# A joint tile of small slot groups in four column groups, and its stream rows gathered first into buffers of their own

## The chip, the cores and the metric

The kernel runs on one core of a Trainium2 chip. A core has TensorE (PE, the matrix unit; its weight loads are listed as PEld), VectorE (DVE), ScalarE (ACT), GpSimd (POOL) and SyncE (SP, which here only issues transfers), and 16 DMA engines that all queues share. Each engine works through its own instructions in order and waits for others by semaphores. The metric is the device time of one execution in microseconds. Before the change the median of three runs is 751.44 us (750.15 to 752.66).

## The reference

The input x holds 16 sequences of 128 tokens of width 256. Two blocks are added to it in turn: a cross-attention, and a feed-forward layer in which each token goes to one of eight experts and to a shared expert. The change touches the second block only. Cut to what matters:

```python
x = x + xcond(ctx_1024, layernorm(x), cond, cond, ...)    # attention, 16 heads of 64
h = layernorm(x)                                           # 2048 tokens of 256
scores = h @ router                                        # one of E = 8 experts, K = 1
vals, idx = top_k(scores, 1)
gates = sigmoid(vals at idx, -inf elsewhere)
routed_in = gates * h                                      # per expert
mid = silu(routed_in @ w1[e]) * (routed_in @ w3[e])        # F = 704
routed_out = mid @ w2[e]
shared = silu(h @ ws1) * (h @ ws3) @ ws2
x = x + shared + routed_out.sum over experts
```

All of it is in f32.

## The kernel before

The program is written with a manual schedule: on every engine, instructions run in the order in which the Python code issues them. Waits between engines, and waits for a buffer's earlier user, are put in by the framework.

The first some 510 us are the attention, with the first units of the shared expert mixed in. Then come the routing and the rest of the shared expert, and from about 585 us the eight expert windows, which the change is about.

**Slots and windows.** The routing (`route`, from L989) counts the tokens of each expert and sorts the experts by load. Window w is the w-th most loaded expert. The program has fixed room for each, in `WINDOWS` (L24): 320, 288, 288, 288, 256, 256, 256, 256 slots. The first 256 slots of a window are two tiles of 128 rows, tiles 2w and 2w + 1. What is over, `REST` = 64, 32, 32, 32 slots for windows 0 to 3, is put together in two joint tiles: tile 16 has window 0's 64 rows (rows 0 to 63), window 1's 32 (64 to 95) and window 2's 32 (96 to 127); tile 17 has window 3's 32 rows alone. The list `rests` (L1194 to L1198) holds for each joint tile the entries (window, first row, number of rows). `table` holds for each tile and row the token in it.

**Inputs.** `gather` (L1200) fetches a tile's rows of h from memory by an indirect DMA that GpSimd issues (tile `xg`, three buffers in the pool `rwork`). `gate` scales them on VectorE. For windows 1 to 7, `turn_inputs` turns them on VectorE in blocks of 32, writes them to memory through SP, and `fetch_inputs` reads them back as columns `xT`. The tiles of window 0 and the two joint tiles are transposed on TensorE instead (`transpose_inputs`, L1215), and VectorE copies the columns to the windows' inputs: one copy for an entry of `rests` (L1225).

**Up.** For each of six chunks f of the hidden width, `up` (L1268) computes the two products `u_w` on TensorE (eight matmul records; the last chunk, `ur_w`, has four), silu on ScalarE, and the product with the other half on VectorE (`mid_w`, L1286). `u_w` has two PSUM buffers, so a chunk can start on TensorE once VectorE's product (L1286) of the chunk two before it is done.

**Down.** `stream_rows` (L1292) gathers, with an indirect DMA of GpSimd, the rows of `s_rows` (x plus the shared expert's part) for a tile's tokens, into the tile `sg`. `out_rows` (L1304) multiplies the hidden tiles by w2 on TensorE (`yr`), six chunks of one matmul for an ordinary tile; for a joint tile each chunk has one matmul for each entry of `rests`, which writes that entry's rows of the output and so uses as many columns of the array (L1310). VectorE adds `sg` (L1313), and GpSimd scatters the rows to the output by an indirect DMA (L1315). Two scatters in a row are ordered: the later one waits for the earlier one to land.

The tile `sg` has the tag `xr` in the pool `mwork`, with three buffers, which the shared expert's tiles `xr` and later the last rows of the output (`held`) use too.

**The order in window w** (L1357 to L1378), all issued behind chunk f = 0 of its up products: the gathers of the stream rows of tiles 2w - 2 and 2w - 1; turning of the next window's inputs; the gathers of h for window w + 2; `down_window(w - 1)`, with its two adds and two scatters; in window 4 (w = `NREST`) `down_rests` for tiles 16 and 17, which issues for each the stream gather, the matmuls, the add and the scatter; then SP's transfers of inputs and weights. Chunks 1 to 5 follow. So GpSimd's queue in window 4 is: stream gathers of tiles 6 and 7, gathers of h for tiles 12 and 13, scatters 6 and 7, stream gather 16, scatter 16, stream gather 17, scatter 17. On VectorE the four adds stand ahead of the product of chunk f = 1.

At the end, `ending` (L1380) does the last eighth of the shared expert and window 7's down products. A second branch, for loads that don't fit the windows, is compiled and is not entered with these inputs.

Of the kernel before, what the change touches and what calls it, by code (L numbers as in the profile page):

```python
# [9 lines left out]
F32 = mybir.dt.float32  # L10
# [7 lines left out]
P = 128  # L18
# [9 lines left out]
def resampler_attn__then__top1_moe_kernel(  # L28
# [17 lines left out]
    nc = tc.nc  # L46
    B, S, D = x.shape
    INNER = wq_t.shape[1]
    E, F = w1.shape[0], w1.shape[2]
# [12 lines left out]
    BL = 32  # L62
# [4 lines left out]
    REST = [n - 2 * P for n in WINDOWS]  # L67
    NREST = sum(r > 0 for r in REST)
    NTILE = 2 * E - (-sum(REST) // P)
# [8 lines left out]
    mwork = ctx.enter_context(tc.tile_pool(name="mwork", bufs=2, side="right"))  # L78
# [176 lines left out]
    def shared_unit():  # L255
        return next(stream, None)
# [653 lines left out]
    rwork = ctx.enter_context(tc.tile_pool(name="rwork", bufs=3))  # L910
# [7 lines left out]
    w2s = [wexp.tile([P, NF, D], F32, name=f"w2_{k}") for k in range(5)]  # L918
# [70 lines left out]
    def route():  # L989
# [191 lines left out]
        for t in first[:3]:  # L1181
            transpose_inputs(t)
# [3 lines left out]
        for t in first[3:]:  # L1186
            transpose_inputs(t)
# [3 lines left out]
    inputs_t = [rwork.tile([P, DC, WMAX], F32, name=f"xT_{k}", bufs=1) for k in range(NREST)]  # L1191
    x_blocks = tc.dram_tile([DC, 2 * NB, BL, NB, BL], F32, name="x_blocks")

    rests = [[] for _ in range(NTILE - 2 * E)]  # L1194
    for w in range(NREST):
        at = sum(REST[:w])
        assert at // P == (at + REST[w] - 1) // P
        rests[at // P].append((w, at % P, REST[w]))  # L1198

    def gather(t, tag="xg"):  # L1200
        xg = rwork.tile([P, D], F32, tag=tag, name=f"xg_{t}")
        nc.gpsimd.indirect_dma_start(
            out=xg,
            out_offset=None,
            in_=h_rows,
            in_offset=Offset(ap=routing["table"][:, t : t + 1], axis=0),
            bounds_check=NT,
            oob_is_err=False,
        )
        xgs[t] = xg  # L1210
# [4 lines left out]
    def transpose_inputs(t, to=None):  # L1215
        xg = xgs.pop(t)
        px = ps_m.tile([P, DC, P], F32, tag="mm", name=f"px_{t}")
        for c in range(DC):
            nc.tensor.transpose(px[:, c, :], xg[:, ts(c, P)], ident)
        if to is None and t < 2 * E:  # L1220
            to = inputs_t[t // 2][:, :, ts(t % 2, P)]
        if to is not None:
            nc.vector.tensor_copy(to, px)
            return
        for w, at, n in rests[t - 2 * E]:  # L1225
            nc.vector.tensor_copy(inputs_t[w][:, :, ds(2 * P, n)], px[:, :, ds(at, n)])

    def turn_inputs(w):

        for i in range(2):  # L1230
            t = 2 * w + i
            gate(t)
            px = rwork.tile([P, DC, NB, BL], F32, tag="xp", name=f"xp_{t}")
            nc.vector.transpose(px, xgs.pop(t).rearrange("p (c k j) -> p c j k", c=DC, k=BL))
            nc.sync.dma_start(
                out=x_blocks[:, ts(i, NB)].rearrange("c i k j q -> (i k) c (j q)"),
                in_=px.rearrange("p c j q -> p c (j q)"),
            )

    def fetch_inputs(w):  # L1240
        for c in range(DC):
            nc.sync.dma_start(
                out=inputs_t[w % NREST][:, c, 0 : 2 * P].rearrange("p (i q) -> p i q", q=BL),
                in_=x_blocks[c].rearrange("i k j q -> (k j) i q"),
            )
# [4 lines left out]
    def load_up(k, w):  # L1250
        e = expert_of(w)
        a1, a3 = (a[ds(e, 1)].rearrange("e (c p) f -> p (e c) f", p=P) for a in (w1, w3))
        nc.sync.dma_start(out=w13s[k][:, :, 0:F], in_=a1)
        nc.sync.dma_start(out=w13s[k][:, :, F : F + FR], in_=a3[:, :, FC * P : F])
        nc.sync.dma_start(out=w13s[k][:, :, F + FR : 2 * F], in_=a3[:, :, 0 : FC * P])

    def load_down(k, w):
        e = expert_of(w)
        a2 = w2[ds(e, 1)]
        nc.sync.dma_start(  # L1260
            out=w2s[k][:, 0:FC, :],
            in_=a2[:, 0 : FC * P, :].rearrange("e (c p) d -> p (e c) d", p=P),
        )
        nc.sync.dma_start(
            out=w2s[k][:, FC, :], in_=a2[:, F - P : F, :].rearrange("e p d -> p (e d)")
        )

    def up(w13, xT, n, mid, f, name):  # L1268

        if f < FC:  # L1270
            ps = ps_s.tile([P, 2, 512], F32, tag="S", name=f"u_{name}_{f}")
        else:
            ps = ps_m.tile([P, 1, 512], F32, tag="mm", name=f"ur_{name}")
        sl = mwork.tile([P, WMAX], F32, tag="sl", name=f"rsl_{name}_{f}")[:, 0:n]
        for k, col in enumerate((f * P, F + FR + f * P) if f < FC else (FC * P,)):
            for c in range(DC):
                nc.tensor.matmul(  # L1277
                    ps[:, k, 0:n],
                    lhsT=w13[:, c, ds(col, P)],
                    rhs=xT[:, c, 0:n],  # L1280
                    start=(c == 0),
                    stop=(c == DC - 1),
                )
        if f < FC:
            nc.scalar.activation(sl, ps[:, 0, 0:n], AF.Silu)  # L1285
            nc.vector.tensor_tensor(mid[:, f, 0:n], ps[:, 1, 0:n], sl, ALU.mult)  # L1286
        else:
            hi = slice(P - FR, P)
            nc.scalar.activation(sl[hi, :], ps[0:FR, 0, 0:n], AF.Silu)
            nc.vector.tensor_tensor(mid[hi, FC, 0:n], ps[hi, 0, 0:n], sl[hi, :], ALU.mult)  # L1290

    def stream_rows(t):  # L1292
        sg = mwork.tile([P, D], F32, tag="xr", name=f"sg_{t}", bufs=3)
        nc.gpsimd.indirect_dma_start(  # L1294
            out=sg,
            out_offset=None,
            in_=s_rows,
            in_offset=Offset(ap=routing["table"][:, t : t + 1], axis=0),
            bounds_check=NT,
            oob_is_err=False,  # L1300
        )
        return sg

    def out_rows(t, parts, sg):  # L1304

        py = ps_m.tile([P, D], F32, tag="mm", name=f"yr_{t}")
        n = max(r.stop for r, _, _ in parts)
        for f in range(NF):
            for rows, mid, wd in parts:
                nc.tensor.matmul(  # L1310
                    py[rows, :], lhsT=mid[:, f, :], rhs=wd[:, f, :], start=(f == 0), stop=(f == NF - 1)
                )
        nc.vector.tensor_tensor(sg[0:n, :], py[0:n, :], sg[0:n, :], ALU.add)  # L1313
        scattered.append(
            nc.gpsimd.indirect_dma_start(  # L1315
                out=out.rearrange("b s d -> (b s) d"),
                out_offset=Offset(ap=routing["table"][0:n, t : t + 1], axis=0),
                in_=sg[0:n, :],
                in_offset=None,
                bounds_check=NT - 1,  # L1320
                oob_is_err=False,
            )
        )
# [13 lines left out]
    mids = [hidden_t.tile([P, NF, WMAX], F32, name=f"mid_w{k}") for k in range(5)]  # L1337
# [3 lines left out]
    def down_window(w, sgs):  # L1341
        for i in range(2):
            out_rows(2 * w + i, [(slice(0, P), mids[w % 5][:, :, ts(i, P)], w2s[w % 5])], sgs[i])

    def down_rests():
        for k, parts in enumerate(rests):
            t = 2 * E + k
            out_rows(
                t,
                [  # L1350
                    (slice(at, at + n), mids[w][:, :, ds(2 * P, n)], w2s[w])
                    for w, at, n in parts
                ],
                stream_rows(t),
            )

    for w in range(E):  # L1357
        for f in range(NF):
            up(w13s[w % 3], inputs_t[w % NREST], WINDOWS[w], mids[w % 5], f, f"w{w}")
            if f == 0:  # L1360
                sgs = [stream_rows(2 * w - 2 + i) for i in range(2)] if w else []
                if w + 1 < E:
                    turn_inputs(w + 1)
                if w + 2 < E:
                    gather(2 * w + 4)
                    gather(2 * w + 5)
                if w:
                    down_window(w - 1, sgs)
                else:
                    shared_unit()  # L1370
                if w == NREST:
                    down_rests()
                if w + 1 < E:
                    fetch_inputs(w + 1)
                if 1 <= w < E - 2:
                    load_up((w + 2) % 3, w + 2)
                if NREST <= w < E - 1:
                    load_down((w + 1) % 5, w + 1)  # L1378
# [138 lines left out]
```

## Time and profile before

| | |
|---|---|
| median of three runs | 751.44 us (750.15 to 752.66) |
| the profiled execution | 750.86 us |
| its span, first to last instruction | 749.1 us |
| granted TensorE clock, mean over the span | 0.997 |
| TensorE busy | 734.9 us, 98% |
| VectorE, ScalarE, GpSimd busy | 383.3, 259.5, 309.9 us |
| all down products of the windows (L1310) | 240 matmul records, from 604.2 to 729.5 us |
| stream gathers (L1294) | 18, landing 2.8, 5.1, 7.5 us after issue (shortest, median, longest) |
| scatters (L1315) | 18, landing 2.0, 2.5, 5.4 us after issue |

How it is read: times are microseconds from the span's start unless marked ns. A line of the timeline has a start, a length, the engine, the line of the kernel, the instruction, output <- inputs, shapes, and a count where several in a row are merged; in brackets stands the idle time of the engine before it and what ended it. `128*64` behind a matmul or weight load is the part of the array that it uses, rows by columns. A matmul in f32 is recorded twice, and its record has some 0.17 us of pipeline behind its own step, so records overlap. A wait for several semaphores is put down to the one that came last.

### The profile page before, as it was taken

Reading aid. Unit: us, or ns where it says so; the run is one execution under the profiler, and the core shown is the slowest. Engines: PE = TensorE matmul, PEld = TensorE weight load, DVE = VectorE, ACT = ScalarE, POOL = GpSimd, SP = SyncE. Lnnn points to the kernel's source line nnn. Section 1 sums busy time; section 2 is a strip of 40 time slices with the busy share of each in tenths; the row PEclk is TensorE's granted clock in tenths of the full one; section 3 lists DMA queues with packets and bytes.
Section 4 is the critical chain, followed back from the end, with each engine's and each line's share of the span. In section 5 each row is a group of like instructions: output and inputs, shape, how many; then the busy total and the mean of one; then the engine's idle time right before and its main releaser. Section 6 shows DMA issues by size and latency. Waiting matters only on the chain. (4 is left out here: it accounts for less than half of the span.)

```text
span 749.1 us, 11455 instructions
## 1 busy us (share of the span) xinstructions
PE 734.9 (98%) x4098; PEld 573.0 (76%) x4098; DVE 383.3 (51%) x948; ACT 259.5 (35%) x787; POOL 309.9 (41%) x363
## 2 busy tenths in 40 slices
PE   8999999999999999999999999999999999989996
PEld 6757768777677677687686788688888778848885
DVE  5566558558647656665655537534633233412321
ACT  2444534544354354344434454711211011101111
POOL 1363553464355445535634644531104333334220
PEclk9999999999999999999999999999999999999999
DMA  8075635844953953863664535551096355564511
GB/s 296 15 250 198 203 127 181 247 150 158 264 169 127 270 195 127 221 227 143 195 195 147 181 127 188 198 164 57 29 331 210 75 145 169 154 181 127 174 35 38
DMA packets 139653, 125.19 MB, mean 167 GB/s; under 512 B 61567, under 2 KB 123522, under 8 KB 139588
## 3 DMA queue, kind: packets, MB, share of 16 engines
q1 hardware_dynamic: 133348, 108.29, 45.7%
q0 software_dynamic: 4224, 12.65, 5.3%
q10 hardware_dynamic: 2016, 3.43, 1.3%
q8 instruction: 34, 0.56, 0.3%
q14 instruction: 31, 0.25, 0.1%
HBM read 75.59 MB, written 48.92 MB: 166 GB/s over the span
## 5 line engine op out<-in xcount | busy, mean ns | idle before, releaser
L530 POOL TENSOR_SCALAR pe<-pe,rs 128x256 f32<-128x256 f32 x256 | 232.6, 929 | 243.8 <-DVE rs L527 243.8
L517 ACT ACTIVATE pe<-S,nmx 128x256 f32<-128x256 f32 x256 | 118.9, 490 | 132.2 <-DVE nmx L510 132.2
L465 PE MATMUL pv<-wv,kvT 128*128 128x512 f32 x256 | 116.5, 599 | 0.2 <-ACT kT L454 0.2
L446 PE MATMUL pk<-kvT,wk 128*128 128x256 f32 x512 | 115.3, 383 | 1.4 <-ACT kT L454 0.7
L446 PEld LDWEIGHTS pk<-kvT,wk 128*128 128x128 f32 x512 | 95.8, 190 | 19.5 <-DVE px L539 2.0
L539 DVE STREAM_TRANSPOSE px<-pe 128x512 f32<-128x512 f32 x128 | 81.4, 682 | 32.2 <-POOL pe L530 32.2
L465 PEld LDWEIGHTS pv<-wv,kvT 128*128 128x128 f32 x256 | 47.2, 190 | 53.2 <-issue 50.6
L1277 PE MATMUL u_w<-xT,w 128*128 128x256 f32 (+2 forms) x320 | 78.9, 402 | 3.3 <-DVE mid_w L1286 3.3
L510 DVE TENSOR_REDUCE nmx<-S 128x4 f32<-128x1024 f32 x64 | 75.0, 1212 | 9.7 <-PE S L498 9.6
L1277 PEld LDWEIGHTS u_w<-xT,w 128*128 128x128 f32 x320 | 61.7, 194 | 17.8 <-DVE mid_w L1286 3.7
L162 PE MATMUL p<-hT,ws 128*128 128x256 f32 x320 | 74.0, 383 | 0.3 <-DVE mid L178 0.2
L162 PEld LDWEIGHTS p<-hT,ws 128*128 128x128 f32 x320 | 59.8, 190 | 10.5 <-DVE mid L178 1.4
L563 PEld LDWEIGHTS O<-pT,v 128*64 128x64 f32 x1024 | 55.2, 137 | 14.7 <-issue 12.9
L498 PE MATMUL S<-kT,qT 64*128 64x256 f32 x512 | 63.9, 389 | 0.0
L563 PE MATMUL O<-pT,v 128*64 128x128 f32 x1024 | 63.0, 276 | 0.0
L472 ACT COPY v<-pv 128x512 f32<-128x512 f32 x64 | 38.2, 599 | 62.9 <-PE pv L465 62.9
L527 DVE RECIPROCAL rs<-sums 128x4 f32<-128x4 f32 x64 | 11.4, 177 | 93.7 <-ACT pe L517 93.7
L579 PEld LDWEIGHTS pw<-wo,oT 128*128 128x128 f32 x256 | 48.6, 190 | 12.2 <-issue 3.1
L579 PE MATMUL pw<-wo,oT 128*128 128x256 f32 x256 | 57.9, 379 | 0.0
L431 PE MATMUL pq<-kvT,wq 128*128 128x256 f32 x256 | 57.7, 379 | 0.0
L1285 ACT ACTIVATE rsl_w<-u_w 128x256 f32<-128x256 f32 (+2 forms) x40 | 16.0, 401 | 119.5 <-PE u_w L1277 119.5
L517 ACT ACTIVATION_READ_ACCUMULATOR pe<-S,nmx 128x1 f32 x256 | 56.5, 221 | 0.0
(218 smaller groups left out, 754.7 us busy)
## 6 DMA issues: line engine op xcount, KB each, us to landing
p_blocks<-px SPq DMA_DIRECT2D x64, 512.0 KB, 2.9
pT<-p_blocks SPq DMA_DIRECT2D x64, 512.0 KB, 4.2
w<-in_w_dram SPq DMA_DIRECT2D x16, 640.0 KB, 7.8
w<-in_w_dram SPq DMA_DIRECT2D x8, 704.0 KB, 5.5
t_blocks<-tx SPq DMA_DIRECT2D x12, 256.0 KB, 2.8
kvT<-t_blocks SPq DMA_DIRECT2D x12, 256.0 KB, 6.1
h_rows<-h SPq DMA_DIRECT2D x8, 256.0 KB, 3.2
xres<-in_x_dram SPq DMA_DIRECT2D x7, 256.0 KB, 4.0
```

The costliest lines, as they stand in the source:

```text
L162: nc.tensor.matmul(ps, lhsT=shared["w13"][:, c, ds(col, P)], rhs=hT[:, c, ts(t, TB)], start=(c == 0), stop=(c == DC - 1),)
L431: nc.tensor.matmul(pq[:, jj], lhsT=wq[:, c, ts(2 * j + jj, P)], rhs=kvTs[g][:, c, :, 1, :], start=(c == 0), stop=(c == DC - 1),)
L446: nc.tensor.matmul(pk[:, jj, :], lhsT=wk[:, c, ts(2 * j + jj, P)], rhs=kvTs[b // 2][:, c, b % 2].rearrange("p t s -> p (t s)"), start=(c = ...
L465: nc.tensor.matmul(pv, lhsT=kvTs[b // 2][:, c, b % 2, t, :], rhs=wv[:, c, ts(n, 512)], start=(c == 0), stop=(c == DC - 1),)
L498: nc.tensor.matmul(pl[:, r, j, :], lhsT=qTs[b // 2][rows, k, b % 2, :], rhs=kTs[b][rows, k, :], start=True, stop=True,)
L510: nc.vector.tensor_reduce(nmx, pl, AX.X, ALU.max, negate=True)
L517: nc.scalar.activation(pes[u][:, h, :], pl[:, r, j, :], AF.Exp, bias=nmx[:, r, j : j + 1], accum_out=sums[u][:, h : h + 1],)
L530: nc.gpsimd.tensor_scalar(w, w, rs[:, i : i + 1], None, ALU.mult)
L539: nc.vector.transpose(px[:, :, t].rearrange("p j h q -> p h j q"), pes[u][:, ts(n, 4), ts(t, S)].rearrange("p h (j k) -> p h j k", k=BL),)
L563: nc.tensor.matmul(o[r * HD : (r + 1) * HD, j, :], lhsT=vs[b][:, t, ts(2 * (4 * half + j) + r, HD)], rhs=pTs[u][:, j // 2, :, t, 2 * (j % ...
L579: nc.tensor.matmul(pw, lhsT=outT[2 * b + k // 4][:, k % 4, :], rhs=wo[:, k, :], start=(k == 0), stop=(k == NP - 1))
L1277: nc.tensor.matmul(ps[:, k, 0:n], lhsT=w13[:, c, ds(col, P)], rhs=xT[:, c, 0:n], start=(c == 0), stop=(c == DC - 1),)
```

## The change

It has two parts. First, an entry of `rests` with more than 32 rows is cut into entries of 32 (`BL`): tile 16 gets four entries of 32 rows in place of 64, 32 and 32; tile 17 stays as it is. Each chunk of tile 16 then has four matmuls of 32 columns, and its input columns are copied in four pieces in place of three. Second, `sg` gets a tag of its own with six buffers in `rwork` (128 x 256, 1 KB a partition each) and leaves the tag `xr` to its other users. The stream gathers of tiles 16 and 17 are issued in window 4 right behind those of tiles 6 and 7, ahead of the turning and the gathers of h, and handed to `down_rests`.

```diff
-        rests[at // P].append((w, at % P, REST[w]))
+
+        rests[at // P] += [(w, at % P + i, 2 * P + i) for i in range(0, REST[w], BL)]
...
-        for w, at, n in rests[t - 2 * E]:
-            nc.vector.tensor_copy(inputs_t[w][:, :, ds(2 * P, n)], px[:, :, ds(at, n)])
+        for w, at, to in rests[t - 2 * E]:
+            nc.vector.tensor_copy(inputs_t[w][:, :, ds(to, BL)], px[:, :, ds(at, BL)])
...
-        sg = mwork.tile([P, D], F32, tag="xr", name=f"sg_{t}", bufs=3)
+        sg = rwork.tile([P, D], F32, tag="sg", name=f"sg_{t}", bufs=6)
...
-    def down_rests():
+    def down_rests(sgs):
         for k, parts in enumerate(rests):
-            t = 2 * E + k
             out_rows(
-                t,
-                [
-                    (slice(at, at + n), mids[w][:, :, ds(2 * P, n)], w2s[w])
-                    for w, at, n in parts
-                ],
-                stream_rows(t),
+                2 * E + k,
+                [(slice(at, at + BL), mids[w][:, :, ds(to, BL)], w2s[w]) for w, at, to in parts],
+                sgs[k],
             )
...
                 sgs = [stream_rows(2 * w - 2 + i) for i in range(2)] if w else []
+                if w == NREST:
+                    rest_sgs = [stream_rows(t) for t in range(2 * E, NTILE)]
...
                 if w == NREST:
-                    down_rests()
+                    down_rests(rest_sgs)
```

## The prediction

> **What bounds the kernel now.** I read the page first, then TensorE's waits behind the attention, then the timelines of TensorE, VectorE and GpSimd around the joint tiles, then the granted clock there. In the page:
>
> ```profile
> span 749.1 us, 11455 instructions
> PE 734.9 (98%) x4098; PEld 573.0 (76%) x4098; DVE 383.3 (51%) x948; ACT 259.5 (35%) x787; POOL 309.9 (41%) x363
> ```
>
> TensorE is busy for 734.9 of 749.1 us. Only a shorter matmul sequence or one of its few gaps can give time. Its waits from 440 us on, in total, count and longest:
>
> ```profile
> PE u_w L1277 <- DVE mid_w L1286: 3.3, 1, 3.3
> PE slots L975 <- DVE at_row L968: 1.1, 1, 1.1
> ```
>
> The one long wait falls in window 4, right behind the joint tiles 16 and 17. TensorE's timeline there (start, length, instruction, idle before):
>
> ```profile
> 651.76 14.30 PE L1310 MATMUL yr<-w,mid_w 128*128 128x256 f32 x72
> 665.99 3.72 PE L1277 MATMUL u_w<-xT,w 128*128 128x256 f32 x16
> 673.05 5.26 PE L1277 MATMUL u_w<-xT,w 128*128 128x256 f32 x16 [3.34 <-DVE mid_w L1286]
> 678.14 1.03 PE L1277 MATMUL ur_w<-xT,w 128*128 128x256 f32 x4
> 680.73 5.34 PE L1310 MATMUL yr<-w,mid_w 128*128 128x256 f32 x24
> 685.91 7.07 PE L1277 MATMUL u_w<-xT,w 128*128 128x256 f32 x32
> ```
>
> An f32 matmul is two records. 24 of them take 5.34 us, the last one's own 0.38 among it: (5.34 - 0.38) / 23 = 0.216 us a record, the step used below. The second row of 16 u_w takes 5.26 us where the first takes 3.72. The table of stretches (length; busy PE, PEld, DVE, ACT, POOL; granted clock; DMA) says why:
>
> ```profile
> 669.70:673.05 3.35, 0.01 (x2) 0.01 (x1) 0.80 (x3) 0.38 (x1) 0.03 (x1) 0.96 0.18 39
> 674.00:675.00 1.00, 1.00 (x4) 0.76 (x3) 0.00 (x0) 0.00 (x0) 0.77 (x1) 0.50 0.04 6
> ```
>
> After 3.3 idle microseconds the clock is 0.50. So the stall costs more than its gap. Its cause, on VectorE and GpSimd:
>
> ```profile
> 657.14 0.42 DVE L1313 TENSOR_TENSOR sg<-yr,sg 128x256 f32<-128x256 f32 x1 [2.17 <-PE yr L1310]
> 666.51 0.42 DVE L1313 TENSOR_TENSOR sg<-yr,sg 128x256 f32<-128x256 f32 x1 [8.95 <-DMA sg<-s_rows,table]
> 672.25 0.41 DVE L1313 TENSOR_TENSOR sg<-yr,sg 32x256 f32<-32x256 f32 x1 [5.32 <-DMA sg<-s_rows,table]
> 672.59 0.73 DVE L1286 TENSOR_TENSOR mid_w<-u_w,rsl_w 128x256 f32<-128x256 f32 x2
> ```
>
> ```profile
> 647.04 1.00 POOL L1202 DMA_INDIRECT xg<-h_rows,table  x1 [0.31 <-issue]
> 658.60 1.01 POOL L1315 DMA_INDIRECT out_dram<-sg,table  x1 [2.27 <-issue]
> 659.91 1.04 POOL L1294 DMA_INDIRECT sg<-s_rows,table  x1 [0.30 <-issue]
> 668.52 1.03 POOL L1294 DMA_INDIRECT sg<-s_rows,table  x1 [0.30 <-issue]
> ```
>
> The rows of tile 16 are gathered at 659.91, behind the scatters of tiles 6 and 7, those of tile 17 at 668.52, behind tile 16's scatter, which waits for its add. VectorE's in-order queue holds the product of f=1 behind both adds.
>
> **Part 1, the gathers moved and given buffers.** Both are now issued behind the gathers of tiles 6 and 7 (644.36 and 645.71), so at 647.04 and 648.4, each some 1.35 us of GpSimd with the pause. They land at most 6.9 us after issue between 640 and 680 us, so by 655.3. Their adds will want them at about 660 and 662.5. What was lost: from 665.99 to 678.14 the 32 u_w records take 12.15 us; in the next window they take 692.82 - 685.91 = 6.91 us. The difference is 5.24, of which 0.10 (an estimate, from the first load behind narrow tiles) stays: **-5.14 us**, 3.34 of it the gap and the rest the slow clock. If the gap goes but the clock falls anyhow, only -3.34; I see no gap left that would lower it. VectorE will not be next: with u_w starting at 662.35 (part 2), f=1's product is done near 665.1, and TensorE needs its buffer at 665.9.
>
> What is queued behind: the gather of tile 12 goes from 647.04 to 649.7; the gather of tile 13 already waits for VectorE until 654.00. Tile 12 is turned only in window 5 (now 681.7). Cost 0, with over 20 us of cover. Later on GpSimd, the scatters run one after another: tile 7's lands at 664.0 (the chain gives it 5.41 us), so tile 16's goes at 664, tile 17's at 667 to 670, and the gathers of tiles 8 and 9 at 668 to 672.5 (now 674.23 and 675.58). Landing within the median to longest, 5.1 to 7.5 us, gives 673 to 680. Their adds, now at 683.54 and 686.11, are wanted 8.6 us earlier, at 674.9 and 677.5. TensorE needs the product behind them at its 17th u_w record, now 685.91 + 16 x 0.216 = 689.4, then 680.8; less the product's 0.42, the adds may end as late as 680.4. So VectorE may wait and TensorE not: cost 0; each microsecond past 680.4 would cost one. Six buffers: each is reused four or more tiles later, long after its scatter. In window 1 the first gather waits 2.41 us for the last store to s_rows; that is data, and stays. The larger pool moves the routing scratch and the hidden tiles up by 6 KB a partition, over tiles of the attention that were last read before the routing begins: 0.
>
> **Part 2, the joint tile as four groups.** The weight loads of tile 16:
>
> ```profile
> 657.03 0.19 PEld L1310 LDWEIGHTS yr<-w,mid_w 128*64 128x64 f32 x2 [0.33 <-issue]
> 657.61 0.14 PEld L1310 LDWEIGHTS yr<-w,mid_w 128*32 128x32 f32 x4 [0.39 <-issue]
> 658.16 0.19 PEld L1310 LDWEIGHTS yr<-w,mid_w 128*64 128x64 f32 x2 [0.41 <-issue]
> 663.26 2.31 PEld L1310 LDWEIGHTS yr<-w,mid_w 128*32 128x32 f32 x16 [0.39 <-issue]
> 665.99 1.16 PEld L1277 LDWEIGHTS u_w<-xT,w 128*128 128x128 f32 x6 [0.41 <-issue]
> ```
>
> A chunk f costs 658.16 - 657.03 = 1.13 us: the 64-column matmul alone takes 0.58, then the two of 32 columns together 0.55. Two records in series are only 0.43; the rest is the array running empty at each change of width. From 657.03 to 665.99 both tiles take 8.96 us. At 663.40 to 663.42 three records are in flight at once:
>
> ```profile
> 663.27 0.42 PE L1310 MATMUL yr<-w,mid_w 128*32 128x256 f32 x3
> ```
>
> They are the two groups of tile 16's last chunk and tile 17's first group: three columns of the array side by side, none later. With four equal groups no width changes, and a chunk is two steps: 12 x 0.216 = 2.59 us for tile 16. Tile 17 has the first group alone, and follows it in series; from 663.26 to 665.99 it takes 2.73 us, start and drain among it. Sum 5.32: **-3.64 us**.
>
> Four at once is not in the trace, so I bound it. Fully parallel: 2.59 us for tile 16. Pairs only: 24 x 0.216 = 5.18. One after another: 48 x 0.216 = 10.37. I take 2.59, nearest to the row of three. The Trainium skill speaks against it in "TensorE: Matmul & The Clock Gate", Measured speedup vs the span model: three column groups gave 2.38 times, not 3. At that efficiency four give 3.17, so 10.37 / 3.17 = 3.27 us and 0.68 less gain. The same page (the section on 56 against 53.3 ns) has an issue cost of about 62 ns a matmul if hardware decoding is off; four groups need one record in 54 ns, so 48 x 0.062 = 2.98. But this row of the attention's two groups has 32 records in 1.97 us, (1.97 - 0.27) / 31 = 55 ns:
>
> ```profile
> 501.77 1.97 PE L563 MATMUL O<-pT,v 128*64 128x128 f32 x32
> ```
>
> The trace decides for both; 0.7 us goes into the range.
>
> **Part 3, one more copy of inputs.** The 64 columns of window 0 become two copies of 32. The three copies now at 576.59 take 0.54 us, four some 0.2 more; the next product starts at 577.28, just behind them, for a buffer that they free. Bounds 0 and 0.3, taken **+0.2**.
>
> **Sum.** -5.14 - 3.64 + 0.2 = -8.6 us. Against the profiled execution, 749.1 becomes 740.5 in span, and 750.86 with what lies around it 742.3. The median shown, 751.44, is 0.6 above that execution: 742.9.
>
> **Rivals.** *Pairs only* (8 in 100): tile 16 takes 5.18, so 745.5. For it: a limit on reads that three groups don't meet; against it: the three in step. *The stall moves* (8 in 100): the gathers of tiles 8 and 9 land past 680.0, TensorE waits some 3.3 us in window 5, and the clock falls again; 5.1 come back: 748.0. For it: GpSimd's scatters wait for each other. Against it: none landed later than 7.5 us. *One after another* (4 in 100): tile 16 takes 10.37, 7.8 more than forecast: 750.7, no difference. *Slower*: each change of group empties the array, as changes of width do. A lone matmul then costs the 0.58 of the 64-column row, 24 of them 13.9 us: 11.3 more, 754.2. It decides from 24 x 0.56 on. Against it: the two 32-column groups that share 0.55 us. 3 in 100.
>
> **How the numbers follow.** The forecast has 77 in 100; its own range is 741.3 (no cost in part 3 and 1.3 us of scatter between executions) to 744.3 (0.7 for the groups, and half of the scatter). The range with the pairs is 741.3 to 746.2; the moved stall and the last two, 15 in 100, stay out. A measurement here tells 0.3%, 2.3 us. Faster: 77 + 8 + 8, less a little for what I don't see, 0.92; same 0.05; slower 0.03.
>
> **What would show it.** TensorE's u_w row of window 4 unbroken with 32 records in about 7.1 us, no clock of 0.50 in the windows; tiles 16 and 17 in 5.3 us, with loads of 32 columns alone and four records in flight; the adds of tiles 16 and 17 waiting for TensorE. A wait of TensorE for mid_w in window 5, or tile 16 above 3.3 us, would make it wrong.

## The result, and the profile after

The changed kernel takes 741.89 us (741.78 to 742.72), the kernel before in the same series 750.85 us (750.15 to 752.66): the ratio is 0.9879, with a 95% interval of 0.9859 to 0.9900. That is 9.0 us less, and the interval reaches from 7.5 to 10.6; forecast were 8.6 less, 742.9. The profiled execution has a span of 740.2 us; 740.5 was forecast.

The page of the changed kernel:

```profile
span 740.2 us, 11477 instructions
PE 728.9 (98%) x4110; PEld 571.2 (77%) x4110; DVE 383.8 (52%) x949; ACT 259.5 (35%) x787; POOL 310.4 (42%) x363
```

TensorE is as full as before, with 12 more matmul records and yet 6.0 us less busy time. The three largest of its waits behind the attention (total, count, longest):

```profile
PE slots L975 <- DVE at_row L968: 1.1, 1, 1.1
PE px L1220 <- DVE mid L178: 0.5, 1, 0.5
PE p L162 <- DVE xT L1227: 0.2, 1, 0.2
```

The wait of 3.3 us for `mid_w` is gone, and one of 0.2 us for the copies of the inputs is new. (Lines behind L1198 have moved by one.) TensorE's timeline in window 4, and under it its weight loads:

```profile
651.47 10.64 PE L1311 MATMUL yr<-w,mid_w 128*128 128x256 f32 x84
662.04 7.17 PE L1278 MATMUL u_w<-xT,w 128*128 128x256 f32 x32
669.05 1.03 PE L1278 MATMUL ur_w<-xT,w 128*128 128x256 f32 x4
```

```profile
656.74 4.89 PEld L1311 LDWEIGHTS yr<-w,mid_w 128*32 128x32 f32 x60 [0.33 <-issue]
662.04 6.77 PEld L1278 LDWEIGHTS u_w<-xT,w 128*128 128x128 f32 x32 [0.41 <-issue]
```

The 32 u_w records are one row of 7.17 us. Tiles 16 and 17 have loads of 32 columns alone. They stand in one row, because no pause parts them, where before there was one of 0.39 or 0.41 us at each change of width. Both tiles take 662.04 - 656.74 = 5.30 us in place of 8.96. On VectorE both adds now wait for TensorE only; on GpSimd the two gathers stand at 646.76 and 648.06, ahead of the gather of tile 12:

```profile
659.63 0.42 DVE L1314 TENSOR_TENSOR sg<-yr,sg 128x256 f32<-128x256 f32 x1 [2.36 <-PE yr L1311]
662.15 0.41 DVE L1314 TENSOR_TENSOR sg<-yr,sg 32x256 f32<-32x256 f32 x1 [2.09 <-PE yr L1311]
```

```profile
646.76 1.00 POOL L1295 DMA_INDIRECT sg<-s_rows,table  x1 [0.30 <-issue]
648.06 1.00 POOL L1295 DMA_INDIRECT sg<-s_rows,table  x1 [0.31 <-issue]
649.37 1.00 POOL L1203 DMA_INDIRECT xg<-h_rows,table  x1 [0.30 <-issue]
```

The measure for the experiments is the stretch of window 4 from TensorE's first down record to its first `ur_w` record, which holds all that the change does in that window. Before it is 678.14 - 651.76 = 26.38 us, after 669.05 - 651.47 = 17.58: 8.80 less.

### The profile page after: what moved, and what is told of

Its sections match the earlier page's. It is cut to its first block, busy times and chain, and to the rows that moved or that the text cites. A ratio compares the mean times of both kernels' runs of the same rounds, so it can differ in the third digit from the quotient of the medians.

```text
span 740.2 us, 11477 instructions
## 1 busy us (share of the span) xinstructions
PE 728.9 (98%) x4110; PEld 571.2 (77%) x4110; DVE 383.8 (52%) x949; ACT 259.5 (35%) x787; POOL 310.4 (42%) x363
## 4 chain that ended last, share of the span: by engine, by line
PE 93%; DVE 3%; ACT 2%; DMA 1%; issue 0%; POOL 0%; ACTq 0%
PE pk L446 15%; PE pv L465 14%; PE u_w L1278 10%; PE S L498 8%; PE O L563 8%; PE p L162 8%; PE pw L579 7%; PE pq L431 7%; PE yr L1311 6%; PE ys L192 5%; PE ur_w L1278 1%; ACT pe L517 1%; PE pr L634 1%; DMA vec<-in_vecs_dram 1%; PE pr L162 1%; PE ys L245 1%
## 5 line engine op out<-in xcount | busy, mean ns | idle before, releaser
L1278 PE MATMUL u_w<-xT,w 128*128 128x256 f32 (+2 forms) x320 | 77.1, 396 | 0.0
L162 PEld LDWEIGHTS p<-hT,ws 128*128 128x128 f32 x320 | 59.8, 190 | 10.6 <-DVE mid L178 1.4
```

Of the source, the lines that this page charges most:

```text
L162: nc.tensor.matmul(ps, lhsT=shared["w13"][:, c, ds(col, P)], rhs=hT[:, c, ts(t, TB)], start=(c == 0), stop=(c == DC - 1),)
L1278: nc.tensor.matmul(ps[:, k, 0:n], lhsT=w13[:, c, ds(col, P)], rhs=xT[:, c, 0:n], start=(c == 0), stop=(c == DC - 1),)
```

## The experiments

Each is a kernel of its own. "Against before" is the ratio to the kernel before on the same chip, with its 95% interval. For this the kernel before was run again beside each group of kernels: its median was 750.48 us for groups_only to filled_gap in the table, 751.93 for one_by_one to loads_ahead, and 750.62 for no_loads. So the ratio counts, not the distance to 750.85. The stretch is that of one profiled execution each.

| kernel | time, us | against before | stretch, us |
|---|---|---|---|
| before | 750.85 | 1 | 26.38 |
| changed | 741.89 | 0.9879 (0.9859 to 0.9900) | 17.58 |
| groups_only | 751.97 | 1.0018 (1.0008 to 1.0027) | 27.00 |
| gathers_only | 746.18 | 0.9951 (0.9935 to 0.9967) | 21.24 |
| gathers_late | 746.67 | 0.9954 (0.9937 to 0.9971) | 22.43 |
| filled_gap | 749.43 | 0.9990 (0.9979 to 1.0001) | 24.82 |
| one_by_one | 746.60 | 0.9936 (0.9917 to 0.9956) | 22.02 |
| tile17_split | 740.20 | 0.9851 (0.9822 to 0.9880) | 15.87 |
| four_buffers | 742.22 | 0.9876 (0.9842 to 0.9911) | 17.58 |
| loads_ahead | 744.67 | 0.9911 (0.9882 to 0.9941) | 20.49 |
| no_loads | 741.46 | 0.9875 (0.9845 to 0.9905) | 17.58 |

The profiled executions of groups_only and one_by_one (754.09 and 749.00 us, the longest of their series) reach window 4 some 2.5 us late. The shift arises before 20 us, in work that no kernel here changes: TensorE waited longer for its first inputs, and its clock was 0.50 for 3.41 us behind that (from 11.54 us in groups_only). The stretch is free of it.

### groups_only: the four groups alone

Against the changed kernel:

```diff
-        sg = rwork.tile([P, D], F32, tag="sg", name=f"sg_{t}", bufs=6)
+        sg = mwork.tile([P, D], F32, tag="xr", name=f"sg_{t}", bufs=3)
...
-                sgs[k],
+                stream_rows(2 * E + k),
...
-                if w == NREST:
-                    rest_sgs = [stream_rows(t) for t in range(2 * E, NTILE)]
...
```

> Four equal groups alone; the rows of tiles 16 and 17 are gathered where they were before, into the three shared buffers. Theory (the late gathers set when window 4 goes on): tiles 16 and 17 take 5.3 us in place of 9.0, but the add of tile 17 still comes at about 672, TensorE's gap in window 4 grows from 3.3 to about 7 us, the 0.50 clock follows it, and the time is 750 to 751.5: the 3.6 us aren't seen. Rival (the two parts add up): 747.2.

Measured: 751.97 us, ratio 1.0018, with an interval that lies above 1. The adds, and TensorE:

```profile
667.86 0.42 DVE L1314 TENSOR_TENSOR sg<-yr,sg 128x256 f32<-128x256 f32 x1 [7.92 <-DMA sg<-s_rows,table]
673.90 0.41 DVE L1314 TENSOR_TENSOR sg<-yr,sg 32x256 f32<-32x256 f32 x1 [5.61 <-DMA sg<-s_rows,table]
```

```profile
654.13 10.64 PE L1311 MATMUL yr<-w,mid_w 128*128 128x256 f32 x84
664.70 3.72 PE L1278 MATMUL u_w<-xT,w 128*128 128x256 f32 x16
674.70 6.59 PE L1278 MATMUL u_w<-xT,w 128*128 128x256 f32 x16 [6.28 <-DVE mid_w L1287]
```

The down products are as fast as in the changed kernel (10.64 us, 3.66 less than before). Of these 3.66 us, 2.94 go into the gap, which grows from 3.34 to 6.28 us; the add of tile 17 comes only 0.72 us earlier in the window. The 16 records behind the gap take 6.59 us, 2.87 more than the undisturbed 3.72; before it was 1.54 more. The clock stays low for longer here. Five microseconds behind the restart it is still 0.50, where the kernel before was back at 0.90 on average in the fourth (columns as in the prediction's table of stretches; groups_only first, then before):

```profile
678.00:680.00 2.00, 2.00 (x7) 1.53 (x6) 0.42 (x1) 0.38 (x1) 1.25 (x2) 0.50 0.28 90
```

```profile
676.00:677.00 1.00, 1.00 (x5) 0.83 (x5) 0.00 (x0) 0.38 (x1) 0.69 (x2) 0.90 0.37 115
```

So 1.33 us of clock outweigh the 0.72, and the stretch is 0.62 us longer than before. The additive rival, 747.2, is out. The half of the change that shortens TensorE's work is worth nothing, or less, without the other.

### gathers_only: the gathers alone

Against the changed kernel, tile 16 has its parts of 64, 32 and 32 again:

```diff
-        rests[at // P] += [(w, at % P + i, 2 * P + i) for i in range(0, REST[w], BL)]
+        rests[at // P].append((w, at % P, REST[w]))
...
```

> Early gathers into six buffers of their own alone; tile 16 keeps its parts of 64, 32 and 32 columns. Theory: the gap of 3.34 us and the slow clock behind it go, tiles 16 and 17 stay at 9.0 us: 750.85 - 5.1 = 745.7. Rival (the stall moves to a later wait): 749 to 751.

Measured: 746.18 us, ratio 0.9951. In the two profiled executions the stretch is 5.14 us shorter than before, to the digit what was forecast for this part. The times show less: the medians differ by 4.3 us, and the ratio says 3.7 (2.5 to 4.9). One reason is given under filled_gap. TensorE:

```profile
651.88 14.30 PE L1311 MATMUL yr<-w,mid_w 128*128 128x256 f32 x72
666.11 7.17 PE L1278 MATMUL u_w<-xT,w 128*128 128x256 f32 x32
```

The down products take the 14.30 us of before, the u_w row is unbroken, and no later wait takes the gap's place. From here to the changed kernel, the four groups bring 21.24 - 17.58 = 3.66 us.

### gathers_late and four_buffers: the place or the buffers

gathers_late keeps groups and buffers and moves the issue:

```diff
-                if w == NREST:
-                    rest_sgs = [stream_rows(t) for t in range(2 * E, NTILE)]
...
-                    down_rests(rest_sgs)
+                    down_rests([stream_rows(t) for t in range(2 * E, NTILE)])
```

> The changed kernel (four groups, six buffers of their own), but both gathers are issued behind the scatters of tiles 6 and 7, ahead of the matmuls of tile 16. Theory (the place in GpSimd's queue counts, not the buffers): issued at about 659.6 and 661, they land at about 666 and 667.5, the add of tile 17 ends near 668.3, and u_w of f=3 starts at about 668.8 in place of 665.5: 741.9 + 3.3 = 745.2, and up to 1.8 more if the clock falls, 747.0. Rival (the shared buffers were what made them late): 741.9.

four_buffers is the changed kernel with `bufs=4` for `sg`.

> The changed kernel with four buffers for the stream rows in place of six. Theory (the place in the queue counts): each buffer is still free when its gather is issued, 741.9. Rival (the depth of six matters): a gather waits for a scatter, and TensorE has a gap again, 744 or more.

Measured: 746.67 and 742.22 us. With six buffers and late gathers the gap is back:

```profile
659.63 1.04 POOL L1295 DMA_INDIRECT sg<-s_rows,table  x1 [0.30 <-issue]
660.98 1.02 POOL L1295 DMA_INDIRECT sg<-s_rows,table  x1 [0.30 <-issue]
```

```profile
668.68 5.41 PE L1278 MATMUL u_w<-xT,w 128*128 128x256 f32 x16 [2.89 <-DVE mid_w L1287]
```

The gap is 2.89 us and the slow clock adds 5.41 - 3.72 = 1.69, both inside what was expected. With four buffers and early gathers the stretch is 17.58 us as with six; against the expectation the second gather waits 0.47 us more for its buffer, which costs nothing. So, with the loads as they are, the place in GpSimd's queue decides, not the depth of six. The early place needs buffers of its own: with three, the gathers of tiles 6, 7, 16 and 17 could not all stand ahead of the scatters that free them. That is argued and was not tried.

### loads_ahead and no_loads: why the late gathers land late

In gathers_late the gathers are issued at 659.63 and 660.98, and their adds start 6.5 and 6.9 us later:

```profile
666.09 0.42 DVE L1314 TENSOR_TENSOR sg<-yr,sg 128x256 f32<-128x256 f32 x1 [8.79 <-DMA sg<-s_rows,table]
667.88 0.41 DVE L1314 TENSOR_TENSOR sg<-yr,sg 32x256 f32<-32x256 f32 x1 [1.36 <-DMA sg<-s_rows,table]
```

Both kernels of this part start from gathers_late. loads_ahead moves 1.4 MB of weights to the head of the window:

```diff
+                if w == NREST:
+                    load_up((w + 2) % 3, w + 2)
                 if w + 1 < E:
                     turn_inputs(w + 1)
...
-                if 1 <= w < E - 2:
+                if 1 <= w < E - 2 and w != NREST:
```

> The kernel of gathers_late (four groups, own buffers, both gathers behind the scatters of tiles 6 and 7) with window 6's up weights (1.4 MB) loaded at the head of window 4, before the turning, so that they are no longer on their way when the gathers are. Theory (the 6.5 us that these gathers take to land is the weights' traffic): they land in 3.6 to 4.7 us, the add of tile 17 ends by about 665.9, TensorE waits under 1 us: 741.9 to 743.5. Rival (they are slow because they follow a scatter in GpSimd's queue): as gathers_late, 746.7.

Measured: 744.67 us, between the two, and so inconclusive. The adds came 4.9 and 5.4 us after the issue of the gathers (661.60 to 666.54, 662.95 to 668.37) in place of 6.5 and 6.9, but the gathers were issued 1.2 us later in the window (9.36 us behind its first down record in place of 8.14), since the scatter of tile 6 ahead of them took 3.7 us to land in place of 2.5. TensorE's gap shrank only from 2.89 to 2.65 us; of the 1.94 us that the stretch is shorter than in gathers_late, 1.69 are the clock, which did not fall this time. The traffic had been moved, not removed. no_loads removes it:

```diff
-                if 1 <= w < E - 2:
+                if 1 <= w < E - 2 and w != NREST:
                     load_up((w + 2) % 3, w + 2)
-                if NREST <= w < E - 1:
+                if NREST < w < E - 1:
                     load_down((w + 1) % 5, w + 1)
```

> The kernel of gathers_late with the weight loads of window 4 left out (window 6's up and window 5's down weights): windows 6 and 5 compute with weights of an earlier window, so this part of the result is another. Theory (these 2.1 MB are what makes the gathers land 6.4 and 6.9 us after issue): the gathers land in about 3.6 us, tile 17's at about 664.6, its add ends at 665.1 at the latest, TensorE has no gap: 741.9. Rival (they are slow because they stand behind a scatter in GpSimd's queue): the gap of 2.9 us stays, 745 to 746.7.

Measured: 741.46 us, stretch 17.58. GpSimd and VectorE:

```profile
660.13 1.04 POOL L1295 DMA_INDIRECT sg<-s_rows,table  x1 [0.30 <-issue]
661.48 1.02 POOL L1295 DMA_INDIRECT sg<-s_rows,table  x1 [0.31 <-issue]
```

```profile
663.12 0.42 DVE L1314 TENSOR_TENSOR sg<-yr,sg 128x256 f32<-128x256 f32 x1 [5.33 <-DMA sg<-s_rows,table]
665.18 0.41 DVE L1314 TENSOR_TENSOR sg<-yr,sg 32x256 f32<-32x256 f32 x1 [1.63 <-DMA sg<-s_rows,table]
```

Behind the same scatter, at the same place of the queue, the gathers serve adds 3.0 and 3.7 us after issue. So the weights of window 4 are what made them late there. A gather that is early enough has time for them: in the changed kernel the two landed 5.1 and 4.2 us after issue, some 8 and 10 us ahead of their adds. In the kernel before, tile 16's gather landed after 6.5 us too; tile 17's landed after 3.6, but was issued late, behind tile 16's scatter. So the stall came of the place and the weights together. How much of it the kernel before would keep without these loads was not tried.

### filled_gap: the price of the slow clock

Against the kernel before:

```diff
         for f in range(NF):
+            if w == NREST and f == 3:
+                fill = ps_o.tile([P, TB], F32, tag="O", name="fill")
+                for _ in range(8):
+                    nc.tensor.matmul(fill, lhsT=ident, rhs=hT[:, 0, 0:TB], start=True, stop=True)
             up(w13s[w % 3], inputs_t[w % NREST], WINDOWS[w], mids[w % 5], f, f"w{w}")
```

> The kernel before, with eight matmuls that nobody reads (16 records, 3.46 us) put between u_w of f=2 and f=3 in window 4, where TensorE stood idle. Theory (the idle gap lowers the clock, which costs 1.8 us beyond the gap): the clock stays at 1.00, f=3 starts at 673.1 as before, and the 16 records behind it take 3.7 us in place of 5.26: 750.85 - 1.6 = 749.2. Rival (the slow clock has another cause, or the measured 5.26 us is only how the records look): 750.9.

Measured: 749.43 us, ratio 0.9990 with an interval that just includes no change; the time alone doesn't settle it. TensorE's timeline does:

```profile
669.73 3.62 PE L1362 MATMUL fill<-hT,ident 128*128 128x256 f32 x16
673.21 3.72 PE L1277 MATMUL u_w<-xT,w 128*128 128x256 f32 x16
```

The u_w records start as late as before, and take 3.72 us in place of 5.26. The granted clock stays at 1.00:

```profile
674.00:676.00 2.00, 2.00 (x11) 1.77 (x10) 0.35 (x1) 0.39 (x1) 1.39 (x3) 1.00 0.02 3
```

The stretch is 1.56 us shorter by work that nobody reads. So the slow clock comes from the idle time, and in the profiled execution it costs about 1.6 us on top of it.

Not every execution of the kernel before pays this. In its profile the clock is 0.50 for 3.41 us, which alone lowers the mean over the span by 0.0023. Yet 9 of the 34 executions run beside this experiment have a mean of 0.999 or 1.000; these take 748.45 to 749.72 us, the other 25 take 749.05 to 752.92. In the 9 the clock cannot have fallen in window 4 for as long. This is one reason why the times of filled_gap and gathers_only show less gain than one pair of profiles does.

### one_by_one: the order of the matmuls

Against the changed kernel:

```diff
-        for f in range(NF):
-            for rows, mid, wd in parts:
+        for rows, mid, wd in parts:
+            for f in range(NF):
```

> The changed kernel with the two loops of the joint tile's matmuls exchanged: all six chunks of one group, then all of the next. The same matmuls in another order. Theory (groups run side by side only if they alternate in TensorE's queue): tile 16 takes 48 records of 0.216 us, 10.4 us in place of 2.6, and both tiles 13.1: 741.9 + 7.8 = 749.7. Rival (TensorE looks far enough ahead to fill the other groups anyhow): 741.9.

Measured: 746.60 us; the stretch is 4.44 us longer than the changed kernel's. The order counts, but the loss is not the 7.8 us expected. The weight loads of both tiles:

```profile
659.36 9.32 PEld L1311 LDWEIGHTS yr<-w,mid_w 128*32 128x32 f32 x60 [0.33 <-issue]
669.09 5.05 PEld L1278 LDWEIGHTS u_w<-xT,w 128*128 128x128 f32 x24 [0.41 <-issue]
```

From the first of them to the load of u_w are 9.73 us, not the 13.1 of a series. If each chain of 12 records runs beside the last four of the chain before, the start of one lies 8 steps behind the start of the last: 4 x 8 x 0.216 + 2.73 = 9.64. In the records a chain does start with the ninth record of the one before it, 1.76 us after that one's start. So a chain in a free group did run beside the one ahead of it, but only beside its last four records. Whether the four depend on the length of the chains or on the f32 type was not tried. Alternating the groups is worth 4.4 us here.

### tile17_split: a version that beats both

After the change, tile 17 is the slow one: one group's 12 records in series while three groups stand idle. Against the changed kernel, in `out_rows` for a tile of 32 rows:

```diff
+        if n == BL:
+            rows, mid, wd = parts[0]
+            for i in range(2):
+                for j in range(3):
+                    f = 2 * j + i
+                    nc.tensor.matmul(
+                        py[ts(j, BL), :], lhsT=mid[:, f, :], rhs=wd[:, f, :], start=(i == 0), stop=(i == 1)
+                    )
+            for j in range(3):
+                nc.vector.tensor_tensor(sg[0:n, :], py[ts(j, BL), :], sg[0:n, :], ALU.add)
+        else:
...
```

> The changed kernel with tile 17's chain cut over three idle column groups: two chunks in each, into rows 0 to 31, 32 to 63 and 64 to 95 of the output, which VectorE adds up with three adds of 32 rows. Theory (tile 17 is bound by its one group's 12 records in series): 4 records in series in place of 12, 8 x 0.216 = 1.7 us less: 741.9 - 1.7 = 740.2. Rival (VectorE's two more adds of 0.41 us hold the product of f=1 and TensorE waits): 741.9.

Measured: 740.20 us (740.18 to 740.31), ratio 0.9851 against before; the changed kernel has 741.78 at its lowest. The stretch is 15.87 us, 1.71 less than the changed kernel's.

```profile
659.40 1.04 PE L1314 MATMUL yr<-w,mid_w 128*32 128x256 f32 x12
660.37 7.17 PE L1278 MATMUL u_w<-xT,w 128*128 128x256 f32 x32
```

Tile 17's 12 records take 1.04 us. VectorE's three adds (1.31 us together) end at 661.8, the product of f=1 runs at 662.81, and TensorE doesn't wait.

## Why the prediction was right

**The gathers (-5.14).** Measured -5.14 in the profile of gathers_only. Both halves are there: the gap (3.34), and the slow clock behind it, which filled_gap takes away alone (1.56). The split was a little off, since the prediction gave the clock all of the rest, 1.80; most of the 0.24 between is the 0.17 us by which a record ends behind its own step, so that the gap costs more than its idle time. That the digit was hit is in part luck: the profile of before happened to be an execution in which the clock fell. By the times this part is worth 3.7 us (2.5 to 4.9). The cause named, the place behind scatters and an add in GpSimd's queue, is shown by gathers_late; that the gathers are also slow there for the weights' traffic, the prediction did not say, and no_loads shows it.

**The four groups (-3.64).** Measured -3.66 between the stretches of gathers_only and the changed kernel. Tiles 16 and 17 take 5.30 us against 5.32 forecast. The trace had three groups side by side at most; four run so too, 48 records in 12 steps of 0.216 us. Two figures of the Trainium skill, in "TensorE: Matmul & The Clock Gate", spoke against it: 2.38 times for three groups (Measured speedup vs the span model), and 62 ns a matmul if hardware decoding is off (Wait — 56ns, not 53.3ns?). The estimates drawn from them, 0.7 and 0.4 us, did not come: the four groups gained 4.0 times over 48 steps in series, with a record every 54 ns. So the first figure does not hold for this kernel, and the second does not apply to it. The rival "pairs only" needed tile 16 at 5.18 us; "one after another" is not even what happens when the order asks for it (one_by_one).

**The copies (+0.2).** Too high. The three copies took 0.54 us; four take 0.61, and TensorE's product stands 0.62 us behind the transpose ahead of it in place of 0.55: +0.07.

**What was costed at nothing.** GpSimd issued the gathers of tiles 8 and 9 at 671.20 and 672.57, at the late end of the 668 to 672.5 given, because tile 16's scatter took 4.8 us to land and tile 17's could go only at 670.00. The adds at 674.46 and 677.02 did not wait for them. There was luck in this: both landed after 2.8 us, not after the 5.1 to 7.5 reckoned with. At 7.5 the second would have landed at 680.1 and its add ended at 680.5, just past the limit of 680.4, so the rival of the moved stall was nearer than it looks. Tile 12's gather went at 649.37 (649.7 forecast).

**The sum.** In the two profiles: window 4 begins 0.29 us earlier (of that +0.07 is the copy's, so 0.36 lies in parts that don't differ), the stretch brings -8.80, and what follows is 0.19 longer: -8.9 in span. In the medians it is -9.0, with an interval of 7.5 to 10.6, so the times can't tell it from the forecast's 8.6; the profiles carry the account.

What the prediction did not say is that its parts depend on each other: it took 3.64 for the groups as their own, and groups_only shows that they bring nothing while the gathers are late. The sum held because the wait was taken away with it.

## What to carry to other kernels

A transfer issued by an in-order queue is as late as what stands ahead of it; where its input has long been ready, issue it ahead of the first instruction that waits, and give it the buffer that this needs. A faster stretch of matmuls in front of a fixed wait only makes the gap longer, so the wait has to go first; and a gap costs more than its length when the clock falls in it or just behind it. Matmuls that use part of the columns ran best here with one width, and alternating between the groups in the queue.

## What the runs showed of the hardware

- Four groups of 32 columns ran side by side without loss: 48 records in 12 steps of 0.216 us. Three had been seen.
- A chain of matmuls in a free column group started only when four records of the chain ahead were left (one_by_one, chains of 12).
- The price of an idle gap in clock was not fixed. The traces record when the granted clock changed:

| run | gap, us | clock 0.50, from and to | next 16 records longer by, us |
|---|---|---|---|
| before | 3.34 (669.71 to 673.05) | 672.78 to 676.20 | 1.54 |
| groups_only | 6.28 (668.42 to 674.70) | 673.72 to 680.55 | 2.87 |
| gathers_late | 2.89 (665.79 to 668.68) | 669.34 to 672.75 | 1.69 |
| loads_ahead | 2.65 (666.52 to 669.17) | did not fall | 0 |

```profile
669.17 3.72 PE L1278 MATMUL u_w<-xT,w 128*128 128x256 f32 x16 [2.65 <-DVE mid_w L1287]
```

  The slow stretches last 3.41 or 6.83 us, and in all eleven traces the time between two changes of the clock is a whole multiple of 3.413 us, for long stretches too (before: 665.60 us, 195 times). In gathers_late the fall comes 0.66 us behind the restart. So the clock changes only at points 3.413 us apart, and where a gap lies between these points seems to bear on its price, not its length alone. In the interval ahead of the fall TensorE idled for 3.07, 3.41 and 2.75 us in the first three runs; the gap of loads_ahead is cut by such a point (reckoned back from a change at 743.03 us) into 1.42 and 1.23 us. What exactly is counted is not shown: in groups_only 1.89 us of idle time in the interval before brought no fall, while near its start, at 11.54 us, some 1.6 us were followed by one. These are one execution each, and no run varies the place of a gap by itself, so no threshold follows. The times agree: all 19 executions of groups_only have a mean clock of 0.995 or less.

- The same indirect gather served its add 3.0 us after issue without the weight loads beside it, and 6.5 us with them.
